# Layer 1's softmax normalised amid the sum of result rows, and the rest's plan at a step's end

## The chip, the cores and the metric

The kernel runs on one core of one Trainium2 chip. The metric is the device time of one launch in microseconds (us), the median of several runs. A profile of one execution on the hardware shows, for each engine of the core, when each instruction began and ended and what it waited for. The engines are PE (TensorE, the matrix unit; PEld is its weight load), DVE (VectorE), ACT (ScalarE), POOL (GpSimd) and SP (SyncE). Each works through its own queue of instructions in order. PE, DVE, ACT and SP get their order from the order in which the kernel's text issues the work; POOL's order is chosen by the scheduler of the kernel's framework.

## The reference

There are 128 graphs of 64 nodes with 256 features, taken as 8192 tokens, and two layers. Each layer is attention over the graph's adjacency followed by a mixture of eight experts, of which each token uses two.

```python
# layer 0
x = x + elu(softmax(where(adj > 0, e, -9e15)) @ Wh)   # Wh = layernorm(x) @ W, e_ij = Wh_i.a1 + Wh_j.a2
x = x + moe0(layernorm(x))                            # router, top 2 of 8, gelu experts 256-256-256
# layer 1
x = x + elu(softmax(where(adj > 0, leaky(e), -9e15)) @ Wh)
x = x + moe1(layernorm(x))                            # router, top 2 of 8, relu experts 256-512-256
```

## The kernel before

The tokens are cut into 16 blocks of 512 (four tiles of 128 rows) in each layer, 32 blocks in all. A block goes through two chains, both written as generators whose `yield`s cut them into stages. The main loop calls the stages one by one, by hand, so that several blocks and the experts' work are interleaved.

`attend` is the attention chain of a block. Its stages in the old kernel are: (1) in layer 1 only, the sum of the two result rows of each token, weighted, onto the token (`xs`, L267, eight DVE instructions for the four tiles and two rows); (2) the layer norm's statistics and the mask; (3) the layer norm's application on ACT (`nb_g`, `xn_g`); (4) the transposes; (5) `wh`, the product with W; (6) `sm2` (L301); (7) the scores `pe` (L309), their maximum and their exponentials with sums on ACT; (8) the reciprocal (L334) and the normalisation (L335); (9) the transposes `pp` (L339) and their copies into `pT_bd`, one half by DVE (L341) and one by ACT (L342); (10) the product `po` (L348); (11) and (12) the ELU and the residual, `xb`.

`route` is the router's chain of a block: the layer norm, the logits, the two largest, the places of the tokens in the experts' lists (`c1` at L458 to `ix` at L494), the writes of the rows into the lists in DRAM by POOL (L499), and in its last stage the plan of the slots. A slot is up to 256 rows of one expert's list. `plan` makes the tables for the full slots that a block completes, on DVE. After the last block of each of layer 0's two parts (blocks 8 and 15) and of layer 1 (block 15), the same stage also calls `fill_up`, which makes SP write eight pads at the lists' ends, and `rests`, which plans what is left of the lists: 33 DVE instructions in all.

The experts' work on a slot has three pieces: `x` transposes the fetched rows (`px`, L764, copied to `xT` by DVE, L768), `h` is the first product (`ph`, L846) with the activation on ACT, and `y` the second (`py`, L877), whose bias is added by DVE (`ys`, L884); then POOL scatters the rows. `py` and `px` have one PSUM buffer each, so the next `py` waits for the bias sum of the one before. The main loop works, at step t, on the attention's stages 4 to 12 of block n = t + 1 and stages 1 to 3 of block t + 2, on the router of block t, and on some four slots. The blocks are numbered through both layers; in this text "block 7 of layer 1" is blocks' number 23.

Of the kernel before, what the change touches and what calls it, by code (L numbers as in the profile page):

```python
# [21 lines left out]
TT = 4  # L22
# [13 lines left out]
def adj_ffn_kernel(  # L36
# [37 lines left out]
    NB = N // TB  # L74
# [51 lines left out]
    for g in range(2):  # L126
        r = slice(g * NG, (g + 1) * NG)
# [132 lines left out]
    def attend(l, b, blk):  # L260

        name = f"g{l}_{b}"
        xs, yb, ai = blk["in"]
        if l > 0:
            for t in range(TT):
                for k in range(2):
                    nc.vector.scalar_tensor_tensor(  # L267
                        xs[:, t, :],
                        yb[:, t, k * D : (k + 1) * D],
                        cs[:, b * TT + t, k : k + 1],  # L270
                        xs[:, t, :],
                        ALU.mult,
                        ALU.add,
                    )
        yield
        stats = ln_stats(xs, name)

        m = work.tile([P, TT, NG], F32, tag="cap", name=f"cap_{name}")
# [123 lines left out]
    def route(l, b, blk):  # L402
# [53 lines left out]
        r = slice(b * TT, (b + 1) * TT)  # L456
# [51 lines left out]
        yield  # L508
        if b - (CUT if b >= CUT and l == 0 else 0) >= LAG:
            slots.take(l, b, SB, plan(l, f"p{l}_{b}", SB))  # L510
        if b == NB - 1 or (l == 0 and b == CUT - 1):
            fill_up(l, b)
            slots.take(l, b, SF, rests(l, f"p{l}_{b}r"), True)
# [21 lines left out]
    def waiting(lf, name):  # L535

        gt = small.tile([P, E, KS], F32, tag="gt", name=f"gt_{name}")
        nc.vector.tensor_tensor(
            gt,
            lf.unsqueeze(2).to_broadcast([P, E, KS]),  # L540
            steps.unsqueeze(1).to_broadcast([P, E, KS]),
            ALU.is_gt,
        )
        ns = small.tile([P, E], F32, tag="ns", name=f"ns_{name}", bufs=3)
        nc.vector.tensor_reduce(ns, gt, AX.X, ALU.add)
        return ns
# [13 lines left out]
    def plan(l, name, n):  # L560

        if done[l] is None:
            du = small.tile([P, E + 1], F32, tag="du", name=f"du_{name}", bufs=3)
            nc.vector.tensor_scalar(du, eidx[:, 0 : E + 1], float(CAP // SL), None, ALU.mult)
            done[l] = du

        lf = small.tile([P, E], F32, tag="lf", name=f"lf_{name}")
        nc.vector.scalar_tensor_tensor(lf, done[l][:, 0:E], -float(SL), base[l], ALU.mult, ALU.add)
        nc.vector.tensor_scalar(lf, lf, float(SL - 1), None, ALU.subtract)
        ns = waiting(lf, name)  # L570
        cum = small.tile([P, E], F32, tag="cum", name=f"cum_{name}")
        summed_up(cum, ns, name)
        ge = small.tile([P, n, E], F32, tag="ge", name=f"ge_{name}")
        nc.vector.tensor_tensor(
            ge,
            cum.unsqueeze(1).to_broadcast([P, n, E]),
            snum[:, 0:n].unsqueeze(2).to_broadcast([P, n, E]),
            ALU.is_le,
        )
        es = small.tile([P, SF], F32, tag="es", name=f"es_{name}", bufs=5)  # L580
        nc.vector.tensor_reduce(es[:, 0:n], ge, AX.X, ALU.add)

        pv = small.tile([P, E], F32, tag="pv", name=f"pv_{name}")
        nc.vector.tensor_tensor(pv, cum, ns, ALU.subtract)
        w = small.tile([P, E], F32, tag="w", name=f"w_{name}")
        nc.vector.tensor_tensor(w, done[l][:, 0:E], pv, ALU.subtract)
        nc.vector.tensor_tensor(
            ge,
            eidx[:, 0:E].unsqueeze(1).to_broadcast([P, n, E]),
            es[:, 0:n].unsqueeze(2).to_broadcast([P, n, E]),  # L590
            ALU.is_equal,
        )
        nc.vector.tensor_tensor(ge, ge, w.unsqueeze(1).to_broadcast([P, n, E]), ALU.mult)
        us = small.tile([P, SF], F32, tag="us", name=f"us_{name}")
        nc.vector.tensor_reduce(us[:, 0:n], ge, AX.X, ALU.add)
        tab = small.tile([P, 2, SF], I32, tag="tab", name=f"tab_{name}", bufs=5)
        nc.vector.tensor_tensor(tab[:, 0, 0:n], us[:, 0:n], snum[:, 0:n], ALU.add)
        nc.vector.tensor_scalar(tab[:, 1, 0:n], es[:, 0:n], float(E - 1), None, ALU.min)
        tk = small.tile([P, E], F32, tag="tk", name=f"tk_{name}")
        nc.vector.tensor_scalar(tk, pv, -1.0, float(n), ALU.mult, ALU.add)  # L600
        nc.vector.scalar_tensor_tensor(tk, tk, 0.0, ns, ALU.max, ALU.min)
        took(l, tk, name)
        return es, tab, sum(written[l], [])
# [85 lines left out]
    class Slots:  # L689
# [173 lines left out]
        def y(self):  # L863
            k = self.ny
            self.weighted()
            if k == self.nh:
                return
            self.ny += 1
            sl = self.all[k]
            l = sl["l"]  # L870
            wc, hT = sl["wc"], sl["hT"]
            py = ps_s.tile([P, ST, D], F32, tag="py", name=f"py_s{k}")
            ys = slot.tile([P, ST, D], F32, tag="ys", name=f"ys_s{k}", bufs=4)
            for w, (_, r) in zip(wc, sl["of"]):
                for t in range(r.start, r.stop):
                    for f in range(HC[l]):
                        nc.tensor.matmul(  # L877
                            py[:, t, :],
                            lhsT=hT[:, f, t * P : (t + 1) * P],
                            rhs=w[:, O2[l] + f * D : O2[l] + (f + 1) * D],  # L880
                            start=(f == 0),
                            stop=(f == HC[l] - 1),
                        )
                nc.vector.tensor_tensor(  # L884
                    ys[:, r, :],
                    py[:, r, :],
                    w[:, OB2[l] : OB1[l]].unsqueeze(1).to_broadcast([P, r.stop - r.start, D]),
                    ALU.add,
                )
            sl["ys"] = ys  # L890
            for t in range(sl["st"]):
                if l == 0:
                    ins = nc.gpsimd.indirect_dma_start(  # L893
                        out=res[sl["part"]],
                        out_offset=self.row(sl, t),
                        in_=ys[:, t, :],
                        in_offset=None,
                        bounds_check=2 * N - 1,
                        oob_is_err=False,
                    )  # L900
                    unordered(f"res{sl['part']}", ins)
            if l == 1:
                self.ready = k
            self.ahead()
# [57 lines left out]
    blks = [{"l": l, "b": b} for l in range(2) for b in range(NB)]  # L962

    def there(i):
        return 0 <= i < len(blks) and blks[i]
# [9 lines left out]
    def a(i, n=1):  # L975
        if there(i):
            for _ in range(n):
                next(blks[i]["a"], None)

    def r(i, n=1):  # L980
        if there(i):
            k = blks[i]
            if "r" not in k:
                k["r"] = route(k["l"], k["b"], k)
            for _ in range(n):
                next(k["r"], None)
# [6 lines left out]
    load(2)  # L993
    load_router()
    load(FIRST)
    a(0, 2)
    make_gw(0)
    a(0)
    a(1, 2)
    token2 = counted("token2", [P, NT], [[2 * P, NT]], 0, 2)  # L1000
    token = counted("token", [P, NT], [[P, NT]], 0, 1)
    place = counted("place", [P, ST], [[P, ST]], 0, 1)
    att = lambda b: [(a, b)] * 9 + [(a, b, 2), (a, b)]
    chains = [
        (0, att(0)[3:] + [(r, 0)] * 10),
        (1, att(1)[2:] + [(r, 1)] * 10),
        (2, att(2) + [(r, 2)] * 9),
        (8, att(3) + [(r, 3)] * 2),
        (12, [(a, 4)] * 3),
    ]  # L1010
    turn = 0
    while any(c for _, c in chains):
# [20 lines left out]
            for l in range(2):  # L1033
                rest_of_lists(l)
        turn += 1
    r(2)
    slots.fetch()
    slots.ahead()
    for t in range(FIRST, len(blks)):
        n = t + 1  # L1040
        more = slots.nf - slots.ny > SB or len(slots.all) - slots.ny > SB
        if t + 3 != NB:
            load(t + 3)
        a(n)
        h()
        x()
        a(n)
        r(t - 1)
        a(n)
        h()  # L1050
        r(t)
        slots.fetch()
        if more:
            x()
        a(n)
        r(t)
        if t + 2 != NB:
            a(t + 2)
        y()
        a(n)  # L1060
        (h if more else x)()
        r(t)
        a(n)
        y()
        a(t + 2, 1 + (t + 2 == NB))
        if more:
            x()
        a(n)
        r(t)
        x()  # L1070
        h()
        a(n)
        if more:
            y()
        x()
        a(n)
        h()
        r(n)
        y()
        a(t + 2)  # L1080
        r(t)
        r(t)
        y()
        slots.fetch()
        x()
        r(n)
        r(t)
        if t + 3 == NB:
            load(t + 3)
    r(len(blks) - 1)  # L1090
    slots.fetch()
    h()
    x()
# [53 lines left out]
```

## Time and profile before

| what | value |
|---|---|
| median of 3 runs | 1414.73 us (1414.56 to 1415.14) |
| the profiled execution's own time | 1416.24 us |
| its span, first to last instruction | 1414.4 us |
| PE busy | 1215.8 us, 86% |
| DVE busy | 872.8 us, 62% |
| POOL busy | 742.8 us, 53% |
| ACT busy | 646.5 us, 46% |
| mean granted TensorE clock | 0.941 |

A row of the view of waits names an instruction with its line, what released it, and then the sum of its waits in us, their number and the longest. A row of the timeline gives the start and the duration in us, the engine, the line, the operation, what it writes and reads, how many instructions are merged into the row, and in brackets the engine's idle time ahead of it with what ended it. A row of windows gives for one stretch of time each engine's busy time, the granted clock of PE as a share of full speed, and the load of the DMA engines. Names carry no buffer numbers: `_g` belongs to the attention, `_r` to the router, `_s` to a slot.

### The profile page before, as it was taken

What the parts mean: (1) busy time and instruction counts of PE and PEld (TensorE: products, weight loads), DVE (VectorE), ACT (ScalarE), POOL (GpSimd) and SP (SyncE); (2) the same over time, 40 slices, a digit from 0 to 9 for tenths busy, and PEclk for the clock granted to TensorE, in tenths of its full rate; (3) what the DMA queues carried; (4) which work ended last, traced back from release to release, by engine and by line L of the source; (5) the groups of instructions that cost most, each with busy time, mean ns of one, the idle gap of its engine ahead of it and who ended that gap; (6) DMA issues with size and microseconds to landing.
All of it is one profiled execution on the core that took longest, in us unless ns stands there. A gap on an engine that the chain in (4) does not pass through costs nothing. (4 is left out here: it accounts for less than half of the span.)

```text
span 1414.4 us, 22289 instructions
## 1 busy us (share of the span) xinstructions
PE 1215.8 (86%) x6240; PEld 1046.3 (74%) x6240; DVE 872.8 (62%) x3390; ACT 646.5 (46%) x1550; POOL 742.8 (53%) x729
## 2 busy tenths in 40 slices
PE   6756799879899887888899999999999999799992
PEld 4645677768787776776788787887878887688882
DVE  3565677877667777767766656766567654523330
ACT  5534556546556544544544454344544444233330
POOL 3153576646666654566545664556645556533323
PEclk9767899989999998999999999999999999999997
DMA  6626567797777978778789887798877777888883
GB/s 198 184 86 191 184 206 235 222 264 235 229 236 222 305 253 249 235 220 273 253 246 265 228 244 202 207 264 228 249 189 216 216 193 205 246 226 227 223 225 34
DMA packets 262829, 311.69 MB, mean 220 GB/s; under 512 B 40615, under 2 KB 219950, under 8 KB 262704
## 3 DMA queue, kind: packets, MB, share of 16 engines
q1 hardware_dynamic: 219552, 225.02, 52.7%
q0 software_dynamic: 43152, 85.24, 22.5%
q8 instruction: 50, 0.82, 0.3%
q14 instruction: 75, 0.61, 0.1%
HBM read 212.25 MB, written 99.75 MB: 221 GB/s over the span
## 5 line engine op out<-in xcount | busy, mean ns | idle before, releaser
L877 PE MATMUL py_s<-wc_s,hT_s 128*128 128x256 f32 x1648 | 402.3, 394 | 31.6 <-issue 22.1
L846 PE MATMUL ph_s<-xT_s,wc_s 128*128 128x256 f32 (+1 forms) x1760 | 384.8, 371 | 19.2 <-DVE xT_s L768 9.1
L877 PEld LDWEIGHTS py_s<-wc_s,hT_s 128*128 128x128 f32 x1648 | 314.4, 197 | 81.6 <-issue 24.8
L922 POOL DMA_INDIRECT out_dram<-ys_s,to_s x135 | 213.2, 1579 | 289.5 <-ACT ys_s L919 150.6
L846 PEld LDWEIGHTS ph_s<-xT_s,wc_s 128*128 128x128 f32 x1760 | 317.6, 192 | 64.1 <-DVE xT_s L768 15.4
L499 POOL DMA_INDIRECT lists<-tn_r,ix_r x256 | 248.8, 972 | 97.0 <-issue 65.8
L855 ACT ACTIVATE hT_s<-ph_s,wc_s 128x256 f32<-128x256 f32 (+1 forms) x440 | 174.5, 456 | 143.5 <-PE ph_s L846 90.6
L884 DVE TENSOR_TENSOR ys_s<-py_s,wc_s 128x512 f32<-128x512 f32 (+1 forms) x149 | 97.3, 653 | 171.2 <-PE py_s L877 170.3
L893 POOL DMA_INDIRECT res<-ys_s,to_s x142 | 144.4, 1017 | 106.7 <-DVE erc_g L334 36.5
L768 DVE COPY xT_s<-px_s 128x512 f32<-128x512 f32 (+1 forms) x140 | 95.3, 681 | 93.4 <-PE px_s L764 93.2
L290 PE MATMUL pw_g<-gw,xt_g 128*128 128x258 f32 x512 | 126.2, 397 | 20.0 <-DVE xt_g L255 13.1
L290 PEld LDWEIGHTS pw_g<-gw,xt_g 128*128 128x128 f32 x512 | 96.6, 197 | 41.3 <-issue 13.0
L919 ACT ACTIVATE ys_s<-ys_s,cf_s 128x256 f32<-128x256 f32 x135 | 61.3, 499 | 104.1 <-DVE ys_s L884 103.9
L240 ACT ACTIVATE tn_r<-xb_g,nb_r,rs_r 128x256 f32<-128x256 f32 x128 | 66.4, 589 | 87.3 <-DVE nb_r L238 87.3
L240 ACT ACTIVATE xn_g<-xs,nb_g,rs_g 128x256 f32<-128x256 f32 x128 | 66.4, 589 | 75.4 <-DVE nb_g L238 75.3
L764 PE MATMUL px_s<-ident,xg_s 128*128 128x128 f32 x554 | 86.9, 281 | 6.4 <-DMA xg_s<-lists 3.7
L764 PEld LDWEIGHTS px_s<-ident,xg_s 128*128 128x128 f32 x554 | 71.3, 147 | 20.2 <-DMA xg_s<-lists 3.8
L279 POOL TENSOR_SCALAR cap_g<-adj 128x256 f32<-128x256 int32 x32 | 35.7, 1116 | 85.8 <-DMA adj<-in_adj_dram 51.7
L348 PE MATMUL po_g<-wh_g,pT_bd 128*128 128x256 f32 x256 | 69.4, 418 | 8.3 <-ACT pT_bd L342 6.8
L297 ACT COPY wh_g<-pw_g 128x258 f32<-128x258 f32 x128 | 47.7, 374 | 58.6 <-PE pw_g L290 57.9
L419 PEld LDWEIGHTS pl_r<-rw,xt_r 128*128 128x128 f32 x512 | 68.8, 209 | 5.3 <-ACT xt_r L257 2.9
L342 ACT COPY pT_bd<-pp_g 64x256 f32<-64x256 f32 x32 | 11.6, 363 | 131.1 <-DVE pT_bd L341 131.0
(503 smaller groups left out, 1612.6 us busy)
## 6 DMA issues: line engine op xcount, KB each, us to landing
wc_s<-in_w_dram SPq DMA_DIRECT2D x142, 512.0 KB, 4.9
wc_s<-in_w_dram SPq DMA_DIRECT2D x156, 256.0 KB, 4.2
xg_s<-lists SPq DMA_DIRECT2D x64, 260.0 KB, 3.2
xg_s<-lists SPq DMA_DIRECT2D x64, 258.0 KB, 4.4
yb<-res SPq DMA_DIRECT2D x16, 1024.0 KB, 12.3
wc_s<-bcat SPq DMA_DIRECT2D x78, 129.0 KB, 4.0
wc_s<-bcat SPq DMA_DIRECT2D x71, 130.0 KB, 5.7
xs<-in_x_dram SPq DMA_DIRECT2D x16, 512.0 KB, 6.2
```

What stands on the lines that cost most here:

```text
L240: nc.scalar.activation(outs(t), xb[:, t, :], AF.Identity, bias=nb[:, t : t + 1], scale=rs[:, t : t + 1])
L290: nc.tensor.matmul(pw, lhsT=xt[:, k, t * P : (t + 1) * P], rhs=gw[l][:, k, :], start=(k == 0), stop=(k == KD - 1),)
L348: nc.tensor.matmul(po[h][:, j, :], lhsT=pT[:, 2 * h + j, :], rhs=wh[:, 2 * h + j, 0:D], start=True, stop=True,)
L499: ins = nc.gpsimd.indirect_dma_start(out=lists[l], out_offset=bass.IndirectOffsetOnAxis(ap=ix[:, k, t : t + 1], axis=0), in_=tn[:, t, 0 : ...
L764: nc.tensor.transpose(px[:, c, t * P : (t + 1) * P], xg[:, t, c * P : (c + 1) * P], ident)
L768: nc.vector.tensor_copy(xT[:, :, 0 : st * P], px[:, :, 0 : st * P])
L846: nc.tensor.matmul(ph[:, j, r], lhsT=w[:, o : o + P], rhs=xT[:, c, r], start=(c == 0), stop=(c == KD - 1),)
L855: nc.scalar.activation(hT[:, f + j, r], ph[:, j, r], AF.Gelu if l == 0 else AF.Relu, bias=w[:, OB1[l] + f + j : OB1[l] + f + j + 1],)
L877: nc.tensor.matmul(py[:, t, :], lhsT=hT[:, f, t * P : (t + 1) * P], rhs=w[:, O2[l] + f * D : O2[l] + (f + 1) * D], start=(f == 0), stop=(f ...
L884: nc.vector.tensor_tensor(ys[:, r, :], py[:, r, :], w[:, OB2[l] : OB1[l]].unsqueeze(1).to_broadcast([P, r.stop - r.start, D]), ALU.add,)
L893: ins = nc.gpsimd.indirect_dma_start(out=res[sl["part"]], out_offset=self.row(sl, t), in_=ys[:, t, :], in_offset=None, bounds_check=2 * N - 1,
L922: ins = nc.gpsimd.indirect_dma_start(out=out, out_offset=self.row(sl, t), in_=ys[:, t, :], in_offset=None, compute_op=ALU.add,)
```

## The change

Stage 1 of `attend` becomes two stages of four instructions each in layer 1 (tiles 0 and 1, then tiles 2 and 3), and two empty stages in layer 0. The loop runs the first half at the old place; where block n belongs to layer 1, it then runs stage 8 of n (the normalisation), then `y`, then the second half of the sum. Where n belongs to layer 0 the normalisation stays behind `y`. The number of calls elsewhere is adapted to the added stage.

In `route` a `yield` parts the plan of the full slots from `fill_up` and `rests`. The added stage is called late in the next step, behind the layer norm's application of block t + 2 and ahead of the router's places of block t. After the last block of layer 1 both stages are called together, as before.

On PE, DVE, ACT and SP no instruction is added or removed. PE's and ACT's orders are the same as before. DVE's order differs in layer 1's steps and at the two moved plans, and SP's at the two `fill_up`s, which now stand behind four fetches and three slots' weight loads. On POOL the order of some neighbours changes: in nine steps of layer 1 the layer norm's power `rs_g` (L232) stands behind both scatters of a slot instead of between them.

```diff
@@ attend
-        if l > 0:
-            for t in range(TT):
+        for i in range(2):
+            for t in range(TT * l * i // 2, TT * l * (i + 1) // 2):
                 for k in range(2):
                     nc.vector.scalar_tensor_tensor(
                         xs[:, t, :],
...
-        yield
+            yield
         stats = ln_stats(xs, name)
@@ route
             slots.take(l, b, SB, plan(l, f"p{l}_{b}", SB))
+        yield
         if b == NB - 1 or (l == 0 and b == CUT - 1):
             fill_up(l, b)
             slots.take(l, b, SF, rests(l, f"p{l}_{b}r"), True)
@@ ahead of the loop
-    a(0, 2)
+    a(0, 3)
     make_gw(0)
     a(0)
-    a(1, 2)
+    a(1, 3)
...
-    att = lambda b: [(a, b)] * 9 + [(a, b, 2), (a, b)]
+    att = lambda b: [(a, b, 2)] + [(a, b)] * 8 + [(a, b, 2), (a, b)]
...
-        (12, [(a, 4)] * 3),
+        (12, [(a, 4, 2), (a, 4), (a, 4)]),
...
-    r(2)
+    r(2, 2)
@@ the loop
         a(n)
         r(t)
+        early = n < len(blks) and blks[n]["l"] == 1
         if t + 2 != NB:
             a(t + 2)
+        if early:
+            a(n)
         y()
-        a(n)
+        if t + 2 != NB:
+            a(t + 2)
+        if not early:
+            a(n)
         (h if more else x)()
         r(t)
         a(n)
         y()
-        a(t + 2, 1 + (t + 2 == NB))
+        a(t + 2, 1 + 2 * (t + 2 == NB))
...
         y()
         a(t + 2)
+        r(t - 1)
         r(t)
         r(t)
         y()
@@ behind the loop
-    r(len(blks) - 1)
+    r(len(blks) - 1, 2)
```

## The prediction

> **What bounds the kernel now.** I read the page first: PE is busy 86% of the span, DVE 62%, and no other engine is near. The chain that ended last begins at 1230 us, after the loop, and says nothing of the steps that the change touches. So the question is what PE waits for in layer 1's steps. The view of waits for PE, cut to 505 to 1180 us, answers:
>
> ```profile
> PE pp_g L339 <- DVE ee_g L335: 31.0, 12, 4.2
> PE pp_g L339 <- DVE l_r L445: 10.9, 4, 3.1
> PE py_s L877 <- issue: 10.6, 15, 1.5
> PE pe_g L309 <- DVE sm_g L301: 5.5, 1, 5.5
> ```
>
> The transposes of the attention weights (pp, L339) wait in all 16 blocks of layer 1, 41.9 us in sum, always until the normalisation (L335) is done. In four blocks the row names the DVE instruction that comes next, L445; it is the same wait. The fourth row is the plan of the rest ahead of sm2. One step by the timeline, block 7 of layer 1:
>
> ```profile
> 801.92 0.60 PE L309 MATMUL pe_g<-sm_g,same 128*128 128x256 f32 x2
> 806.19 3.74 DVE L267 SCALAR_TENSOR_TENSOR xs<-yb,cs,xs 128x256 f32<-128x256 f32 x8
> 808.03 0.60 PE L764 MATMUL px_s<-ident,xg_s 128*128 128x128 f32 x4
> 809.85 0.68 DVE L884 TENSOR_TENSOR ys_s<-py_s,wc_s 128x512 f32<-128x512 f32 x1
> 810.65 0.42 DVE L335 TENSOR_TENSOR ee_g<-ee_g,erc_g 128x256 f32<-128x256 f32 x1
> 811.22 0.60 PE L339 MATMUL pp_g<-ident,ee_g 128*64 128x128 f32 x4 [2.59 <-DVE ee_g L335]
> 811.66 3.62 PE L877 MATMUL py_s<-wc_s,hT_s 128*128 128x256 f32 x16
> 813.51 0.41 DVE L341 COPY pT_bd<-pp_g 64x256 f32<-64x256 f32 x1
> 813.95 0.36 ACT L342 COPY pT_bd<-pp_g 64x256 f32<-64x256 f32 x1 [7.75 <-DVE pT_bd L341]
> 815.32 0.69 DVE L884 TENSOR_TENSOR ys_s<-py_s,wc_s 128x512 f32<-128x512 f32 x1 [1.40 <-PE py_s L877]
> ```
>
> PE is done with px at 808.63. The exponentials ended at 806.2, but DVE goes through eight row sums (3.74 us) and a bias sum (0.68) first. DVE has no idle time from 803.4 until L341 ends at 813.92; po (L348) starts at 815.11, when py is through, 0.80 us after its second operand came (L342 ends 814.31). That 0.80 matters most below.
>
> **Part 1: normalisation amid the sum.** Nothing is added or removed: the DVE order of a layer-1 step becomes four sums, reciprocal and normalisation, bias sum, four sums; PE and ACT keep their order. Half the sums take 1.87 us, so the reciprocal can start at 806.19 + 1.87 = 808.06, the normalisation ends 0.62 later (810.45 to 811.07 in the trace) at 808.68, and pp starts at 808.83 instead of 811.22. The bias sum frees py at 809.36, as pp ends. So PE's gap shrinks by 2.4 us.
>
> Not all of it is kept. L341, which makes po's operand, stands behind both halves of the sum as before; DVE has the same work up to it and no idle time, so it ends at 813.92 again, and po can't start before 814.36. What is late next is therefore po on L342: the step gains 815.11 - 814.36 = 0.75 us, not 2.4, and PE shows about 1.4 us idle ahead of po. After po, DVE has 1.40 us of idle time ahead of its next bias sum and 3.77 ahead of the one after, so it follows PE, and the 0.75 is kept.
>
> I did the same for all 16 blocks: the lesser of the pp gap and of the time from L342's end to po, less 0.05 (the least seen between them).
> - Blocks 6, 7, 9, 11, 13 (0.80 us each between L342 and po): 5 x 0.75 = 3.75.
> - Blocks 8, 10, 12, 14 (2.30, 2.27, 2.13, 2.22): 8.7. Here py ran at half clock after the gap.
> - Blocks 2, 4, 5 (2.19, 1.98, and a gap of 1.84): 2.1 + 1.9 + 1.8 = 5.8.
> - Block 0 (1.01): 0.96. Block 1 (0.14): 0.1. Block 15 has no sum, but its normalisation passes the bias sum, for which DVE sat idle 2.0 us: 0.8.
> - Block 3: 0. There py is in two parts and the second waits for a bias sum behind L341 (0.70 us in the trace); the gap just moves to it.
>
> Sum 20.1 us.
>
> **The clock.** Rows of PE's work in windows as long as the shortest slow stretch:
>
> ```profile
> core 0: us, PE busy (x) PEld busy (x) DVE busy (x) ACT busy (x) POOL busy (x), PEclk, DMA share, GB/s
> 851.20:854.60 3.40, 1.14 (x8) 0.78 (x6) 3.26 (x9) 0.00 (x0) 0.00 (x0) 1.00 0.96 275
> 854.60:858.00 3.40, 3.08 (x10) 2.55 (x11) 2.78 (x14) 0.35 (x1) 0.00 (x0) 0.50 0.73 224
> 806.80:810.20 3.40, 1.83 (x11) 1.39 (x9) 3.29 (x8) 0.00 (x0) 0.11 (x1) 1.00 1.01 284
> 246.40:249.80 3.40, 2.42 (x16) 2.06 (x15) 3.01 (x12) 1.07 (x3) 1.97 (x2) 1.00 0.50 107
> ```
>
> A window with PE busy 1.14 of 3.40 us is followed by one at clock 0.50; with 1.83 busy it is not. So a gap of 2.6 us costs a slow stretch when it falls inside a window, which is why every other block has one. The Trainium skill ("TensorE: Matmul & The Clock Gate", HAM oscillation) puts the limit at idle gaps above some 3.4 us. By that rule the gaps of 2.6 us would be harmless, blocks 8, 10, 12, 14 would be slow for another reason and gain only about 0.75 each, and the sum would be 20.1 - 5.7 = 14.4. The trace decides: I keep 20.1. Its limit also speaks for new losses: in blocks 0, 1 and 3 the remaining gap (ahead of po, or of py's second part) is about 4.7, 3 and 3 us, enough for a slow stretch of 3.4 us, up to 1.7 us each. Two of these blocks have one now, ahead of po, where it costs less. I take off 2 us: 18.
>
> **POOL and SP.** In nine steps POOL's rs (L232) of the later block moves behind a second scatter of 1.6 us: it ends about 1.85 us later, at 828.55 where block 7's nb_g started at 828.45. DVE then stalls up to 0.8 us there, but has 1.06 us idle ahead of its next bias sum and ACT's xn some 1 us ahead of PE: cost 0, and up to 0.8 x 9 = 7 us if this cover is gone. Weight loads on SP wait for bias sums, which come earlier.
>
> **Part 2: the rest's plan.** Only the plans after layer 0's blocks 8 and 15 move; the last one keeps its place. Each is 33 DVE instructions, 7.2 us (300.20 to 307.41; 547.17 to 554.24), then SP's eight list fills (8.35 us). PE around the first:
>
> ```profile
> 301.25 1.04 PE L251 MATMUL pt_r<-ident,tn_r 128*128 128x128 f32 x8
> 307.88 1.22 PE L309 MATMUL pe_g<-sm_g,same 128*128 128x256 f32 x2 [5.59 <-DVE sm_g L301]
> 309.75 3.42 PE L419 MATMUL pl_r<-rw,xt_r 128*128 128x8 f32 x16
> 333.95 1.99 PE L846 MATMUL ph_s<-xT_s,wc_s 128*128 128x256 f32 x8 [0.59 <-DVE xT_s L768]
> ```
>
> The old place costs a 5.6 us gap and then a slow clock: from pp to pp this step takes 40.2 us, the one before 30.1, so 10.1. At the new place, behind nb_g (329.90), DVE has no idle time up to xT (333.21), for which ph already waits 0.59. All 7.2 us therefore fall on that ph, with a gap of 7.8 us; what PE can still do (py, px, pt) is before it. Behind the plan on DVE also stand block 9's list places (L458 to L494), and so POOL's eight list writes, 7 us later; their rows are fetched two steps on. A gap that long brings the slow clock too; behind the 7.44 us gap ahead of ph at 1237 it lasted 3 us, so I add 2 us. 10.1 - 9.2 = about 1 us gained. For block 15's plan: with the plan gone pe starts near 549.1, DVE's unbroken chain from there to xT sets ph, and with 7.2 us back in it ph comes at 581.0 instead of 583.07; less 2 us for the clock, 0. On SP the fetch of four slots goes ahead of the fills and one weight load behind them; the fetch of the rest's slots comes at the step's end as before (335.67), 3 us or more after the fills, and in the loop's steps no PE wait on a fetch is seen past 170 us. Bounds for part 2: from -8 us (the plan hidden after all) to +8 us (both long gaps with 10 us of slow clock, as after 305 us).
>
> **Sum.** The profiled execution took 1416.24 us (span 1414.4), 1.5 above the median. 18 + 1 = 19 less: 1397.2 for that one, 1395.7 against the median of 1414.73; I say 1396.
>
> **Rivals.**
> 1. *The plan costs more at its new place* (0.12). For: no cover there. Against: the old place was as bare. +8 us: 1404.
> 2. *Slower, by the clock gate* (0.10). The 1.4 us left ahead of po could bring a slow stretch into each step, now in dense work: 1.7 us x 13 blocks = 22 against 19 gained, 1418. It decides from 12 such blocks on. Against: layer 0's steps have gaps of 0.98 and 0.55 us close together (the window at 246.40, 2.42 us busy) and run at full clock from 176 to 305 us; 1.4 idle of 3.4 leaves 2.0 busy, above the 1.83 that stayed fast.
> 3. *The copy L341 does not hold po* (0.05): then the whole 41.9 us, less some 4, goes, 1377 at the extreme; halfway 1386. Against: ACT's L342 waits for it in all 16 blocks.
> 4. *Nothing moves* (0.04): the gap reappears whole at po, as in block 3. For: that is what DVE's order suggests for blocks 1 and 3. Against: the measured 0.8 to 2.3 us elsewhere.
>
> **Numbers.** The forecast has 0.69. Below it alone 1389 to 1404; with rival 1, part of 3 and the bounds of part 2 the range is 1387 to 1409. A measurement here tells about 0.2% (2.8 us) from no change: faster 0.85, same 0.05, slower 0.10.
>
> **What would show it.** After: pp's wait for L335 falls from 41.9 us to below 6; a new wait po on ACT L342 of 1 to 1.5 us per block, 20 us or more in sum; no slow clock in blocks 6 to 14; pe's waits for sm2 (5.59, 5.50) gone and a wait of about 7.8 us on xT at ph twice. Wrong if po doesn't wait, if slow stretches appear in most layer-1 steps, or if rs delays nb_g enough to reach ph.

## The result and the profile after

| | before | after |
|---|---|---|
| median, first measurement | 1414.93 us (4 runs, 1414.56 to 1415.5) | 1396.6 us (4 runs, 1392.18 to 1398.88) |
| ratio, 95% interval | | 0.9867 (0.9846 to 0.9889) |
| median on another chip (19 runs of before, 7 of after) | 1416.53 us | 1394.22 us, ratio 0.9839 (0.9813 to 0.9866) |
| profiled execution, its span | 1416.24, 1414.4 us | 1392.18, 1390.4 us |
| mean granted clock | 0.941 | 0.952 |

The change takes 18 us off by the first pair of medians, 22 by the second. The profiled execution of after is the quickest of the first four; it is 24 us below that of before.

First the view of waits for PE from 505 to 1180 us, the same view as in the prediction. (In the new kernel the lines of slots and router are one higher: L877 is L878, L768 is L769, L884 is L885.)

```profile
PE po_g L348 <- ACT pT_bd L342: 19.7, 13, 2.8
PE py_s L878 <- issue: 10.3, 16, 1.5
PE ph_s L847 <- DVE xT_s L769: 9.1, 3, 7.5
PE pp_g L339 <- DVE ee_g L335: 7.2, 13, 1.8
```

The wait of pp on the normalisation has gone from 41.9 to 7.2 us, and more than half of what it lost is back under another name, po on L342, 19.7 us. The third row is the moved plan of layer 0's last block, 7.5 us of the 9.1. Block 7 of layer 1 again, by the timeline, from its pe on:

```profile
791.19 0.60 PE L309 MATMUL pe_g<-sm_g,same 128*128 128x256 f32 x2
795.55 1.92 DVE L267 SCALAR_TENSOR_TENSOR xs<-yb,cs,xs 128x256 f32<-128x256 f32 x4
797.30 0.60 PE L765 MATMUL px_s<-ident,xg_s 128*128 128x128 f32 x4
797.59 0.42 DVE L335 TENSOR_TENSOR ee_g<-ee_g,erc_g 128x256 f32<-128x256 f32 x1
797.94 0.68 DVE L885 TENSOR_TENSOR ys_s<-py_s,wc_s 128x512 f32<-128x512 f32 x1
798.16 0.60 PE L339 MATMUL pp_g<-ident,ee_g 128*64 128x128 f32 x4 [0.27 <-DVE ee_g L335]
798.54 1.91 DVE L267 SCALAR_TENSOR_TENSOR xs<-yb,cs,xs 128x256 f32<-128x256 f32 x4
798.67 3.72 PE L878 MATMUL py_s<-wc_s,hT_s 128*128 128x256 f32 x16
802.88 0.41 DVE L341 COPY pT_bd<-pp_g 64x256 f32<-64x256 f32 x1
803.33 0.36 ACT L342 COPY pT_bd<-pp_g 64x256 f32<-64x256 f32 x1 [7.86 <-DVE pT_bd L341]
803.74 2.00 PE L348 MATMUL po_g<-wh_g,pT_bd 128*128 128x256 f32 x8 [1.35 <-ACT pT_bd L342]
```

pp follows the normalisation after 0.27 us of idle time instead of 2.59. But L341 still ends where DVE's queue lets it, 4.5 us after pp is done, behind the second half of the sum and the router's instructions. py is through at 802.39; po starts 0.05 us after L342 ends, with PE 1.35 us idle. From pe to po the block takes 12.55 us now. Before, with pe at 801.92, it took 13.19:

```profile
815.11 1.89 PE L348 MATMUL po_g<-wh_g,pT_bd 128*128 128x256 f32 x8
```

### The profile page after: what moved, and what is told of

Same layout as the page of the kernel before. It is cut to its first block, busy times and chain, and to the rows that moved or that the text cites. A ratio compares the mean times of both kernels' runs of the same rounds, so it can differ in the third digit from the quotient of the medians.

```text
span 1390.4 us, 22289 instructions
## 1 busy us (share of the span) xinstructions
PE 1202.5 (86%) x6240; PEld 1031.3 (74%) x6240; DVE 872.4 (63%) x3390; ACT 647.1 (47%) x1550; POOL 741.9 (53%) x729
## 5 line engine op out<-in xcount | busy, mean ns | idle before, releaser
L878 PE MATMUL py_s<-wc_s,hT_s 128*128 128x256 f32 x1648 | 391.4, 386 | 32.4 <-issue 20.7
L878 PEld LDWEIGHTS py_s<-wc_s,hT_s 128*128 128x128 f32 x1648 | 305.1, 191 | 81.3 <-issue 23.4
L885 DVE TENSOR_TENSOR ys_s<-py_s,wc_s 128x512 f32<-128x512 f32 (+1 forms) x149 | 97.1, 651 | 147.6 <-PE py_s L878 146.1
L769 DVE COPY xT_s<-px_s 128x512 f32<-128x512 f32 (+1 forms) x140 | 95.4, 682 | 96.3 <-PE px_s L765 96.2
L290 PEld LDWEIGHTS pw_g<-gw,xt_g 128*128 128x128 f32 x512 | 96.7, 197 | 41.6 <-issue 13.2
L348 PEld LDWEIGHTS po_g<-wh_g,pT_bd 128*128 128x128 f32 x256 | 51.3, 211 | 44.9 <-ACT pT_bd L342 35.0
L342 ACT COPY pT_bd<-pp_g 64x256 f32<-64x256 f32 x32 | 11.7, 364 | 125.7 <-DVE pT_bd L341 125.6
```

The lines of the kernel that those rows point to most:

```text
L290: nc.tensor.matmul(pw, lhsT=xt[:, k, t * P : (t + 1) * P], rhs=gw[l][:, k, :], start=(k == 0), stop=(k == KD - 1),)
L348: nc.tensor.matmul(po[h][:, j, :], lhsT=pT[:, 2 * h + j, :], rhs=wh[:, 2 * h + j, 0:D], start=True, stop=True,)
L769: nc.vector.tensor_copy(xT[:, :, 0 : st * P], px[:, :, 0 : st * P])
L878: nc.tensor.matmul(py[:, t, :], lhsT=hT[:, f, t * P : (t + 1) * P], rhs=w[:, O2[l] + f * D : O2[l] + (f + 1) * D], start=(f == 0), stop=(f ...
L885: nc.vector.tensor_tensor(ys[:, r, :], py[:, r, :], w[:, OB2[l] : OB1[l]].unsqueeze(1).to_broadcast([P, r.stop - r.start, D]), ALU.add,)
```

## The experiments

The theory: of the 2.6 us per block that pp waited, what is kept is only what L341 allows, since po waits for L341's copy through L342; the plan's move is worth about nothing. Rivals: the gain is due to the plan's move; L341 isn't what holds po; more idle time ahead of po turns into half clock.

**1. Part 1 alone.** The second `yield` in `route` and the added call are left out.

```diff
-        yield
         if b == NB - 1 or (l == 0 and b == CUT - 1):
...
-        r(t - 1)
```

> Part 1 alone: the normalisation amid the sum, both moved plans back ahead of sm2. My account: part 1 carries nearly all of the gain, 18 to 19 us of the 18.3, so 1396 to 1398; in the profile the two waits of pe for sm2 (5.6 and 5.5 us) are back, the two waits of ph for xT of about 7.5 us are gone, po waits for L342 about 1.35 us in nine blocks. Rival (the plan's move gives a good part): this kernel stays at 1402 to 1408.

Measured: 1399.23 us (1397.78 to 1401.03), ratio 0.987 (0.985 to 0.9891). The waits from 505 to 1180 us:

```profile
PE po_g L348 <- ACT pT_bd L342: 21.0, 13, 2.8
PE pe_g L309 <- DVE sm_g L301: 5.6, 1, 5.6
PE pp_g L339 <- DVE ee_g L335: 5.3, 12, 1.6
```

Part 1 alone gives the ratio of the change, within the intervals. The plan's wait is at its old place, pe on sm2.

**2. Part 2 alone**, that is, before with those two lines and the matching counts ahead of the loop and behind it.

> Part 2 alone: the two plans moved to the step's end, the order of sum and normalisation as before. My account: 0 to 2 us faster than before, 1413 to 1415, with pe's waits for sm2 gone and two new waits of ph for xT of 7 to 8 us; pp's 41.9 us of waits in layer 1 as before. Rival (the move frees what it was meant to free): 5 to 11 us faster, 1404 to 1410. Second rival (no cover at the new place and a longer slow clock): 3 to 8 us slower.

Measured: 1419.48 us (1413.63 to 1426.18), ratio 1.0002 (0.9985 to 1.0019).

```profile
PE pp_g L339 <- DVE ee_g L335: 33.1, 12, 4.3
PE pp_g L339 <- DVE l_r L445: 11.1, 4, 3.2
PE ph_s L847 <- DVE xT_s L769: 8.1, 2, 7.5
```

The plan's 5.5 us ahead of pe has become 7.5 ahead of ph, and the time stays. The two rows of pp have 44.2 us together where before has 41.9: in block 1 of layer 1 pp waits 4.28 us instead of 2.06 (more of this in the point on pp's remaining wait below). The change's gain is part 1's.

**3. The second half of the sum behind L341.** If L341 holds po, the half must stand behind it.

```diff
         y()
-        if t + 2 != NB:
-            a(t + 2)
         if not early:
             a(n)
         (h if more else x)()
         r(t)
         a(n)
+        if t + 2 != NB:
+            a(t + 2)
         y()
```

> The changed kernel with the second half of the sum moved on DVE from behind the bias sum to behind the copy L341; PE and ACT keep their order. My account (the copy, standing behind the second half, holds po): L341 comes 1.87 us earlier, po's wait of about 1.35 us goes in nine blocks, and so do up to 1.87, 1.3, 1.8 and 1.6 us in blocks 0, 1, 2 and 4; block 3 keeps its wait. 15 to 19 us faster than the changed kernel, 1378 to 1382. Rival (what the change was worth is pp's gap, and po waits for something else): no change, 1396. Second rival (the delayed bias sum of the second y then holds the next py, or the later row sum holds the layer norm): 1390 to 1400.

Measured: 1381.9 us (1379.0 to 1383.34), ratio 0.9735 (0.9716 to 0.9754), 17.3 us below part 1 on the same chip.

```profile
PE py_s L878 <- issue: 12.4, 16, 1.5
PE ph_s L847 <- DVE xT_s L769: 11.5, 7, 7.5
PE pp_g L339 <- DVE ee_g L335: 6.1, 10, 1.8
PE po_g L348 <- ACT pT_bd L342: 1.9, 2, 1.0
```

po's wait falls from 21.0 to 1.9, and the time by nearly as much. In the blocks numbered 22 to 30 the steps now take 41.3 to 41.6 us, where part 1 alone and the changed kernel take 43.1 and before took 43.7 in those without half clock: the 2.4 us of the pp gap are now nearly all gained. That shows that L341's place on DVE held po, and that the prediction's "0.75 us, not 2.4" was the price of that place alone.

**4. Three quarters of the sum first, one behind the normalisation.**

```diff
-            for t in range(TT * l * i // 2, TT * l * (i + 1) // 2):
+            for t in range(3 * l * i, 3 * l + l * i):
```

> The changed kernel with the sum cut 3 tiles to 1 instead of 2 to 2: the normalisation comes 0.94 us later, pp's wait grows by about 0.94 us in each block with a sum, L341 stays where it is. My account (L341 ends the step's first half): same time as the changed kernel within 2 us, po's wait falls by what pp's wait grows. Rival (each us of pp's wait costs a us): 0.94 x 15 = 14 us slower than the changed kernel, 1411.

Measured: 1393.8 us (1392.71 to 1397.77), ratio 0.9832 (0.9812 to 0.9852).

```profile
PE pp_g L339 <- DVE ee_g L335: 21.1, 15, 2.9
PE po_g L348 <- ACT pT_bd L342: 7.9, 13, 1.9
```

The two waits are exchanged: 29.0 us together, where the changed kernel has 26.9. DVE's work up to L341 is the same wherever the sum is cut, so the cut only decides at which of the two PE stands; the rival's 14 us are not there. The blocks numbered 21 to 30 took 433.1 us here and 432.1 both in the changed kernel and with part 1 alone. The median is 5 us below part 1's on this chip. The profiled executions, only 1.2 us apart, don't explain it: blocks 15 to 20 took 3.1 us less here (226.4 against 229.5), and these blocks differ by more than that between two executions of one kernel, as the table below shows.

**5 to 7, first time.** The next three kernels were run on a chip where before itself took 1647.01 us (1637.41 to 1658.55).

> The half moved behind pp's copy, as in the run before (1381.9 us), and besides that the plan of the rest is cut into pieces of 4 to 13 VectorE instructions, placed in gaps of VectorE one and two steps later instead of in one piece at the end of a step; TensorE's and ScalarE's order is that of the run before. My account: each of the two plans costs TensorE about 9.2 us there (7.2 to 7.5 us of ph's wait for xT, and about 2 us of half clock behind it); in pieces about 0 to 1, so 15 to 17 us less: about 1366 us. Rival A: the pieces make late what the step needs (xT, sm2), 1 to 2 us for each of them: 1372 to 1378. Rival B: the plan's wait is covered by something else that is late at the same place (the slot's rows fetched late, px waits for them): no gain or a few us, 1378 to 1384.

> The changed kernel with one more VectorE instruction of about 0.48 us (128x256, on constants, into a buffer that nobody reads) ahead of the copy that po waits for, in every block of layer 1: po's gap of 1.35 us becomes about 1.83. My account: 13 to 15 blocks pay 0.48 each, +6 to +7 us, about 1403 to 1406, and the clock is as before, since TensorE's busy share of a 3.41-us window about the gap stays above the 0.41 to 0.46 under which half clock followed. If the copy does not hold po: no change.

> The changed kernel with two such instructions, po's gap about 2.3 us. Linear account: +0.96 in 13 to 15 blocks, +12.6 to +14, about 1410, with no more half clock than in the changed kernel. Clock account: the gap now takes the busy share of some windows of 3.41 us under 0.46, and half clock follows for a window in about half of the blocks, about 1.7 us each: +20 to +24, about 1417 to 1420. The run with one such instruction is the control: it has the delay and not the half clock.

Measured: 1639.07 us, ratio 0.9944 (0.9919 to 0.9969); 1663.03, 1.0078 (1.0048 to 1.0109); 1668.84, 1.011 (1.0074 to 1.0145). The first rows of the waits of PE over the whole span of the second of them tell why these say little:

```profile
PE pw_g L290 <- ACT wh_g L297: 58.7, 12, 10.0
PE pw_g L290 <- issue: 51.2, 12, 9.3
PE pl_r L423 <- DVE xt_r L255: 46.7, 13, 5.8
```

In nearly every step PE stands still for 4 to 10 us at a place where it waits for next to nothing on the other chips, so what the experiments change is hidden or not beside that. Engine times of single instructions are as elsewhere (the bias sum 690 ns, the copy xT 687). What holds that chip up isn't settled; the trace has no landing times of its DMAs. The three were run again, with the changed kernel beside them:

> The changed kernel itself, timed beside the three runs that follow it, on their chip: 1392 to 1399 us and 0.987 of before if the chip is like the one of the first measurement; on a chip like the one where before took 1647 us, about 20 us under before.

Measured: 1394.22 us (1390.67 to 1403.07); before 1416.53. The profiled execution of this run took 1403.07, its slowest.

**5. The plan of the rest in pieces**, on top of experiment 3. `rests` becomes a generator with three `yield`s between its parts, and its update of the lists' ends moves into the first part; `route` has a stage for each, and the loop calls them in DVE's gaps one and two steps later.

```diff
-            slots.take(l, b, SF, rests(l, f"p{l}_{b}r"), True)
+            pieces = rests(l, f"p{l}_{b}r")
+            next(pieces)
+            yield
+            next(pieces)
+            yield
+            next(pieces)
+            yield
+            slots.take(l, b, SF, next(pieces), True)
...
         h()
+        r(t - 2)
         x()
         a(n)
+        r(t - 2)
         r(t - 1)
         a(n)
+        have = len(slots.all)
+        r(t - 2)
+        if len(slots.all) > have:
+            slots.fetch()
+            more = True
+        r(t - 1)
         h()
```

> The kernel with the half behind pp's copy and the rest's plan in pieces of 4 to 13 VectorE instructions, once more, beside the changed kernel on the same chip (the first time before took 1647 us on its chip, not 1415 to 1418). My account: about 1366 us where before takes 1415 to 1418, that is 0.965 of before and 30 us under the changed kernel (15 for the half behind the copy, 15 to 17 for the two plans). Rival A (pieces make xT and sm2 late, 1 to 2 us each): 1372 to 1378, 0.969 to 0.974. Rival B (something else is late at the plan's place): 1378 to 1384, 0.974 to 0.978, as with the half behind the copy alone.

Measured: 1365.21 us (1363.63 to 1370.53), ratio 0.965 (0.9623 to 0.9676), 29 us below the changed kernel on the same chip. The ph behind the first plan, in the timeline of the changed kernel:

```profile
330.37 3.78 PE L847 MATMUL ph_s<-xT_s,wc_s 128*128 128x256 f32 x8 [7.44 <-DVE xT_s L769]
```

The same ph with the pieces:

```profile
323.52 1.99 PE L858 MATMUL ph_s<-xT_s,wc_s 128*128 128x256 f32 x8 [0.55 <-DVE xT_s L780]
```

From pe to the next pe the step with the first plan takes 30.5 us (experiment 3: 39.9), that with the second 33.7 (43.0): 9.4 us for each plan, where 9.2 was reckoned. Of the two steps behind each plan one is 1.1 us longer than in experiment 3 (37.3 against 36.2, block 12): PE's waits there are the same, but it has two windows of half clock instead of one, as before the change has. The others are no longer, so the pieces themselves are free; both rivals fall. This version is faster than both kernels of the case.

**6 and 7. L341 later by one and by two instructions.** The diff is that of one; the other has `2 * l`.

```diff
+        for i in range(1 * l):
+            nc.vector.scalar_tensor_tensor(
+                idle[:, 0:SL], places, nhalf[:, 0:1], places, ALU.mult, ALU.add
+            )
         nc.vector.tensor_copy(pT[0:NG, :, 0:NG], pp[:, :, 0:NG])
```

> The changed kernel with one more VectorE instruction of 0.48 us ahead of the copy that po waits for, in every block of layer 1, once more, beside the changed kernel. My account: +6 to +7 us against the changed kernel (0.995 of before), no more half clock than there. If the copy does not hold po: no change.

> The same with two such instructions. Linear account: +12.6 to +14 us against the changed kernel (about 0.996 to 1.0 of before), no more half clock than there. Clock account: half clock follows po's gap for a window of 3.41 us in about half of the blocks, +20 to +24 us against the changed kernel (1.001 to 1.005 of before).

Measured: 1408.49 us (1403.77 to 1409.37), ratio 0.994 (0.9919 to 0.9961), and 1418.14 us (1409.97 to 1423.14), ratio 1.0002 (0.9981 to 1.0022): 14.3 and 23.9 us above the changed kernel. The expectation for one instruction was too low by half; that for two came out in its sum by the clock account, but not where it put it. Two stretches of the loop, from pe of block 15 to pe of block 21 and from there to pe of block 31, in the views of windows of each kernel (length in us, granted clock):

| kernel | blocks 15 to 20 | blocks 21 to 30 |
|---|---|---|
| before | 231.5, 0.93 | 445.7, 0.98 |
| after | 226.0, 0.95 | 432.1, 1.00 |
| after, another execution | 233.9, 0.93 | 432.3, 1.00 |
| part 1 alone | 229.5, 0.94 | 432.1, 1.00 |
| the half behind L341 | 228.4, 0.95 | 417.1, 1.00 |
| one instruction more | 237.0, 0.93 | 435.9, 1.00 |
| two instructions more | 243.1, 0.90 | 444.7, 0.99 |

In blocks 21 to 30 the delay is seen nearly alone: po's gap in the blocks numbered 22 to 30 goes from 1.35 to 1.74 and 2.26 us (an instruction of 0.48 us takes 0.4 to 0.5 of DVE's time in a row of others), and one instruction costs 3.7 us there, two 12.5. The second step of that is larger because two of these blocks now get half clock. Windows of two blocks of the kernel with two instructions, in the columns that the prediction explains:

```profile
775.24:778.65 3.41, 1.45 (x7) 0.94 (x5) 3.13 (x16) 0.12 (x1) 0.00 (x0) 1.00 0.80 277
778.65:782.06 3.41, 3.11 (x16) 2.77 (x17) 3.24 (x12) 2.83 (x8) 2.04 (x2) 1.00 0.54 135
819.61:823.02 3.41, 1.14 (x6) 0.66 (x5) 3.17 (x14) 0.48 (x2) 0.00 (x0) 1.00 0.71 253
823.02:826.43 3.41, 3.41 (x8) 2.61 (x9) 2.23 (x10) 1.39 (x3) 2.43 (x2) 0.50 0.58 174
```

and po in these blocks, by the timeline:

```profile
778.95 1.99 PE L352 MATMUL po_g<-wh_g,pT_bd 128*128 128x256 f32 x8 [2.26 <-ACT pT_bd L346]
822.93 3.68 PE L352 MATMUL po_g<-wh_g,pT_bd 128*128 128x256 f32 x8 [2.27 <-ACT pT_bd L346]
```

The gap is the same to a hundredth. In the second block it lies wholly in one window of 3.41 us, 1.14 us of PE's work are left there, and the next window runs at 0.50: po takes 3.68 us instead of 1.99. In the first it is parted between two windows and nothing follows. Such a step takes 45.7 us, one without 44.0. With one instruction the least busy window of these blocks has 1.68 us of work, and no half clock follows in any:

```profile
814.08:817.50 3.42, 1.68 (x8) 1.17 (x7) 3.18 (x15) 1.05 (x3) 0.00 (x0) 1.00 0.74 263
```

So the clock account holds, but for blocks 22 to 30 it was put too high (two blocks of nine, not half of them). The rest is in blocks 15 to 20, where gaps of 1.5 to 7.5 us stand close together and half clock comes and goes from one execution to the next: the two executions of the changed kernel differ there by 7.9 us. By the records of the clock, PE had half clock for 20.5 and 30.7 us of these blocks in those two executions, for 34.1 us with one instruction more and 47.8 with two. What the one instruction cost there beyond its delay of some 2 us can't be told from one profile of each; by the medians it is 8 to 9 us. That this is half clock is likely from these times, but argued, not shown.

## Why the prediction came true, point by point

The time, 1396, was right, and so was its sum in the main. That it lies within 1 us of the first median is in part luck: on the other chip the gain was 22 us instead of 18, and executions of the changed kernel alone spread over 7 us on the first chip and 12 on the other. The steps from one pe to the next in the two profiles against its terms:

| term of the sum (us gained) | predicted | profile |
|---|---|---|
| blocks 2 to 5 of layer 1 | 5.8 | 6.2 |
| blocks 6, 7, 9, 11, 13, "0.75 each" | 3.75 | 3.5 |
| blocks 8, 10, 12, 14 | 8.7 | 8.1 |
| blocks 0 and 1 with the second plan, 1.06, less 2 for the clock | -0.9 | 0.9 |
| block 15 | 0.8 | 1.0 |
| layer 0, with the first plan | 1 | 2.7 |
| behind layer 1's blocks | 0 | 1.5 |
| sum | 19 | 24 |

- **L341 sets po.** "The step gains 0.75 us, not 2.4" is what the profile shows (0.65 in blocks 7, 9 and 13), and experiment 3 shows the cause. The third rival, that L341 does not hold po, is refuted.
- **po's new wait**, "1 to 1.5 us per block, 20 us or more in sum": 1.35 in the blocks numbered 22 to 30, 1.34 to 2.80 in four of the first five, 19.7 in sum in this execution and 21.0 in the other.
- **Half clock gone from the dense blocks.** Blocks 8, 10, 12 and 14 gained 2.0 us each, three times the others; the changed kernel has no half clock in blocks 22 to 30. The Trainium skill's limit ("TensorE: Matmul & The Clock Gate", HAM oscillation: idle gaps above some 3.4 us), which the prediction set aside, would have allowed 0.75 there. Experiment 7 shows the same by itself: a gap of 2.27 us is enough.
- **pp's remaining wait**, "below 6": 7.2. The surplus is block 1 of layer 1, where pp still waits 1.84 us, and it is part 2's doing, which the sum of part 1 left out. Before, the plan's gap ahead of that block's pe brought half clock, the eight py ahead of pp took 3.76 us, and so pp waited only 2.06. With the plan moved they take 1.97 and PE is at pp early. Experiment 1, with the plan at its old place, has no wait there and 5.3 in sum; experiment 2 has 4.28 there.
- **The loss to the clock in blocks 0, 1 and 3**, "I take off 2 us". The idle time came as reckoned, "about 4.7, 3 and 3 us", though in two blocks it is parted: 1.67 ahead of pp and 2.80 ahead of po in block 0, 1.84 and 1.34 in block 1, 2.87 ahead of py's second part in block 3. In the profiled execution half clock follows at 523 us behind po's gap and at 554 behind that of pp. Block 3's gap is free there: two windows share it, busy for 1.64 and 1.88 us. In the other execution one window holds the same gap (3.04 us), 0.37 us of work are left in it, and half clock follows at 643.9. (Both, and before, have half clock behind two later gaps of block 3, 1.49 and 1.87 us.) What the half clock costs depends on the execution. In the profiled one nothing is lost against before, which has half clock about these places too; in the other execution blocks 15 to 20 take 7.9 us more.
- **Part 2**, "about 1 us gained": experiment 2 gives 1.0002 of before, so 0 within about 3 us. The waits came as named, 7.44 and 7.50 us at ph (7.8 reckoned), and pe's 5.59 and 5.50 gone. That a plan costs 9.2 us at the new place was confirmed by experiment 5 (9.4).
- **Surplus of the profiled execution.** It is 24 us below before's, 5 more than the sum. Of these about 2 are the term for the clock just named, 1.7 are in layer 0 outside the plan, and 1.5 come from one stretch of half clock at 1199 us in before, which after does not have. These are windows that fall otherwise from one execution to the next, and the medians, 18 and 22 us apart, lie about the sum.
- **rs behind a second scatter** cost nothing, as reckoned: from 505 to 1180 us ph waits for xT only 1.6 us besides the plan's 7.5.

## What to carry to other kernels

When an instruction is brought forward on an in-order engine, follow the chain to the next instruction of the same engine that the waiting one needs: here the normalisation moved by 2.3 us, but the copy behind it stood still. Of block 7's 2.3 us only 0.65 were kept; the rest came back one product later. The gain was to be had by putting the movable work behind the last instruction of the chain, not into its middle. A block of small instructions that nobody needs soon, such as the plan, is best cut into pieces the size of the engine's own gaps: moving it whole only moved its wait.

## What was not expected of the hardware

- Half clock comes in stretches of whole windows of 3.41 us. In the traces of before, after (both executions) and the two delays, each window but the first of the span in which PE is busy for less than 1.4 us (0.41 of it) is followed by half clock, whatever the length of the gap; 2.27 us of idle time are enough if one window holds them all, and the same gap is free if two windows share it. Above that, busy time doesn't separate the windows: in the changed kernel one with 1.57 us of work was followed by half clock, and in experiment 7 one with 1.45 was not:

```profile
550.58:553.99 3.41, 1.57 (x12) 1.09 (x11) 3.27 (x9) 0.00 (x0) 1.27 (x2) 1.00 0.06 9
553.99:557.40 3.41, 3.10 (x8) 1.93 (x6) 3.16 (x12) 0.00 (x0) 1.98 (x2) 0.50 0.87 233
```

- What counts may be the columns that PE moves, not the time in which it is busy. The window ahead of the half clock at 1199 us in before is busy for 3.06 of 3.41 us, but two thirds of that are 16 products of the router's logits (L419), which move 8 columns each:

```profile
1197.11 2.06 PE L419 MATMUL pl_r<-rw,xt_r 128*128 128x8 f32 x16 [0.35 <-DVE xt_r L255]
1199.03 5.39 PE L877 MATMUL py_s<-wc_s,hT_s 128*128 128x256 f32 x16
```

  If each product counts for its columns alone, at 216 ns for 256 (the usual distance between ph's products at full clock), that window has 1.0 us of work. This is an estimate, made on the ten traces from the chips at 1415 to 1418 us, past 130 us: so counted, the 124 windows at full clock that half clock followed have at most 1.39 us of work, and the 3337 others at least 1.29. By busy time the same two groups reach up to 3.12 and down to 1.37. No run was made to test it.

- The windows run free of the program: within each trace every change of the clock lies on one grid of 3.41 us, to 3 ns, and in the two executions of the changed kernel this grid's first line falls 1.03 and 2.16 us behind the first instruction. Those two took 226.0 and 233.9 us over the same six blocks, and 432.1 and 432.3 over the ten dense ones. That is 7.9 of the 10.9 us by which they differ, and a reason to compare kernels by their dense stretches.
- Chips differ by far more than the change is worth: before took 1414.93, 1418.3 and 1416.53 us on three occasions and 1647.01 on another chip, with stalls of 4 to 10 us in nearly every step. Ratios from there are no measure of what a step gains.
